# Channel sums on GpSimd ahead of one averaging product, in the inner norm of a retention layer

## The chip, the core and the metric

The kernel runs on one core of a Trainium2 chip. The core has five engines that run side by side and meet at semaphores: TensorE (PE, matrix products into PSUM), VectorE (DVE), ScalarE (ACT), GpSimd (POOL) and SyncE (SP, which issues the DMAs of the activations and the FFN weights here). PE's weight loads are shown apart as PEld. The metric is the time of one execution on the device in microseconds.

## The reference

One layer of attention without softmax ("retention"), and one FFN, each between two norms ("sandwich"). x has 4 x 1024 tokens of 512 channels, all in float32.

- Attention: `xn = layernorm(x)`; q, v and the gate are `xn` times three 512x512 matrices; the state runs along the sequence, `state = lam * state + v`; then `out = q * state`.
- The inner norm, which the change is about: over the 512 channels of each token, `mu = mean(out)`, `var = mean((out - mu)^2)`, `out = (out - mu) * rsqrt(var + 1e-5) * gamma + beta`.
- Then `out * silu(gate)`, a product with Wo, and `x = x + layernorm(that)`.
- FFN: `xn = layernorm(x)`; gate and up project to 1536 with weights rounded to float8 values and scaled per output; `silu(gate) * up` goes back to 512 by a third such matrix; `x = x + layernorm(that)`.

## The kernel before

The 4096 tokens are worked in eight blocks (t = 0 to 7) of 512 tokens, `TB`. Within attention the data lies transposed: channels on the 128 partitions, in NC = 4 chunks, and the 512 tokens of the block along the free dimension. So a chunk of one block is a 128x512 tile.

`retention(t)` is a generator; each `yield` ends a step. Its steps are: two for the first norm and the transposes into `xnT` (L218 to L228), four for the chunks (L232 to L247), one for mu and its subtraction (L248 to L253), one for var and the reciprocal root (L254 to L262), four for the gate (`wg`) and the scaling (L265 to L275), and five for the output projection `po`, the residual and the next norm (L279 to L298). In the step of a chunk c, PE makes `pv` and `pq` (`project`, L200, four products each), DVE scans `pv` along the tokens (L237), keeps the last column in `carry` (L245) and multiplies by `pq` into `y[:, c, :]` (L246).

The mean over channels is a mean over partitions and over the four chunks. It is taken on PE: `mean_w` is a 128x128 matrix filled with 1/512, and the product of it with a chunk puts the chunk's share of the mean on all 128 partitions; the four chunks add up in one PSUM tile:

```python
for c in range(NC):
    nc.tensor.matmul(mu, mean_w, y[:, c, :], start=(c == 0), stop=(c == NC - 1))
```

DVE subtracts mu from the four chunks (L252). For var, ACT squares each chunk into a tile `sq` (L257) and PE takes the same product of it (L258). ACT takes the root of var (L260), which needs a load of another activation table before it and one after it, and DVE the reciprocal (L261).

`ffn(t)` has NI = 12 steps, one for each 128 of the 1536 hidden channels. In a step PE makes the gate and the up product (`project_split`, L209, eight passes each: the input is split into two float32r parts), ACT the silu (L320), DVE the product with up (L321), ACT and DVE split the result into two parts (the cast L323 and the subtraction L324, into `fuse`), and PE then makes the down product of the step before (L310, eight passes). After the twelve steps come the norm and the residual (L332 to L335, with the add on POOL at L334).

`together` weaves the generators: ffn(t) runs its thirteen steps, and after each of them retention(t + 1) makes so many of its seventeen that it ends with the twelfth; that puts the last chunk and mu behind the same FFN step, and var behind the next. retention(0) runs alone. A third generator, `round_weights`, rounds the FFN weights in twelve pieces with DVE and ACT (L148 to L157, 128x1536 each); six pieces go with retention(0), six with ffn(0) and retention(1). From these calls the Tile framework's scheduler makes the final order of each engine's instructions, which can differ from the order of the calls, and puts in the semaphore waits. [...]

Buffers that matter: PSUM has a pool `ps_a` with two banks, in which pv, pq, mu, var, the gate and po take turns, and a pool `ps_f` with two for the FFN's gate and up. In SBUF the tag `ret` has two buffers, for the scan's output and for `sq`; the tag `rstd` has one, for the reciprocal root of a block (read last at L270). POOL has little work: the tiny operations that make a reciprocal root of the token norms (`rstd_of`, L168 and L169) and the two residual adds (L293 and L334).

Of the kernel before, what the change touches and what calls it, by code (L numbers as in the profile page):

```python
# [10 lines left out]
F32 = mybir.dt.float32  # L11
I32 = mybir.dt.int32
F32R = mybir.dt.float32r
AF = mybir.ActivationFunctionType
ALU = mybir.AluOpType

P = 128
# [5 lines left out]
def retention_ffn_sandwich(  # L23
# [19 lines left out]
    nc = tc.nc  # L43
    NT, D = x.shape
    I = gate_w.shape[1]
    NC = D // P
    NI = I // P
    TB = 512
# [7 lines left out]
    work = ctx.enter_context(tc.tile_pool(name="work", bufs=2))  # L56
    small = ctx.enter_context(tc.tile_pool(name="small", bufs=4))
    ps_a = ctx.enter_context(tc.tile_pool(name="ps_a", bufs=2, space=bass.MemoryType.PSUM))
# [59 lines left out]
    mean_w = const.tile([P, P], F32, tag="mean_w", name="mean_w")  # L118
# [42 lines left out]
    def stats(src, mv):  # L161
        st = small.tile([P, 6], F32, tag="st", name="st")
        nc.vector.bn_stats(st, src)  # L163
        nc.vector.bn_aggr(mv, st)  # L164

    def rstd_of(var, n):
        r = small.tile([P, n], F32, tag=f"rstd{n}", name="rstd")
        nc.gpsimd.tensor_scalar(r, var, EPS, 1.0, ALU.add, ALU.mult)  # L168
        nc.gpsimd.tensor_tensor(r, r, nhalf[:, :n], ALU.pow)  # L169
        return r  # L170

    def center_scale(dst, src, mean, rstd):
        nc.vector.tensor_scalar(dst, src, mean, rstd, ALU.subtract, ALU.mult)  # L173

    def norm(dst, src):
        mv = small.tile([P, 2], F32, tag="mv", name="mv")
        stats(src, mv)
        rstd = rstd_of(mv[:, 1:2], 1)
        center_scale(dst, src, mv[:, 0:1], rstd)

    def to_channels(dst, src, s):

        pt = ps_a.tile([P, NC, P], F32, tag="pa", name="pt")
        for c in range(NC):
            nc.tensor.transpose(pt[:, c, :], src[:, ts(c, P)], ident)
        nc.scalar.copy(dst[:, :, ts(s, P)], pt)

    def to_channels_split(hi, lo, src, s):

        pt = ps_a.tile([P, NC, P], F32, tag="pa", name="pt")  # L190
        for c in range(NC):
            nc.tensor.transpose(pt[:, c, :], src[:, ts(c, P)], ident)
        nc.scalar.copy(hi[:, :, ts(s, P)], pt)  # L193
        nc.vector.tensor_tensor(lo[:, :, ts(s, P)], pt, hi[:, :, ts(s, P)], ALU.subtract)  # L194

    def project(pool, tag, w, col, xT):

        po = pool.tile([P, TB], F32, tag=tag, name=f"po_{tag}")
        for c in range(NC):
            nc.tensor.matmul(  # L200
                po, w[:, c, ts(col, P)], xT[:, c, :], start=(c == 0), stop=(c == NC - 1)
            )
        return po
# [11 lines left out]
    def retention(t, give):  # L215
        xt = xs[t]

        mv4 = small.tile([P, NS, 2], F32, tag="mv4", name="mv4")  # L218
        for s in range(NS):
            stats(xt[s], mv4[:, s, :])  # L220
        rstd4 = rstd_of(mv4[:, :, 1], NS)
        xnT = big.tile([P, NC, TB], F32, tag="xnT", name=f"xnT_{t}")
        for s in range(NS):
            xn = work.tile([P, D], F32, tag="tok", name=f"xn_{t}_{s}", bufs=5)
            center_scale(xn, xt[s], mv4[:, s, 0:1], rstd4[:, s : s + 1])
            to_channels(xnT, xn, s)
            if s % 2 == 1:
                yield  # L228


        y = big.tile([P, NC, TB], F32, tag="y", name=f"y_{t}")
        for c in range(NC):  # L232
            pv = project(ps_a, "pa", wv_sb, c, xnT)
            pq = project(ps_a, "pa", wq_sb, c, xnT)
            ret = work.tile([P, TB], F32, tag="ret", name=f"ret_{t}_{c}")
            first = (t * TB) % seq == 0
            nc.vector.tensor_tensor_scan(  # L237
                ret,
                lam[:, c : c + 1].to_broadcast([P, TB]),
                pv,  # L240
                0.0 if first else carry[:, c : c + 1],
                ALU.mult,
                ALU.add,
            )
            nc.vector.tensor_copy(carry[:, c : c + 1], ret[:, TB - 1 : TB])  # L245
            nc.vector.tensor_tensor(y[:, c, :], pq, ret, ALU.mult)  # L246
            yield  # L247
        mu = ps_a.tile([P, TB], F32, tag="pa", name=f"mu_{t}")  # L248
        for c in range(NC):
            nc.tensor.matmul(mu, mean_w, y[:, c, :], start=(c == 0), stop=(c == NC - 1))  # L250
        for c in range(NC):
            nc.vector.tensor_tensor(y[:, c, :], y[:, c, :], mu, ALU.subtract)  # L252
        yield  # L253
        var = ps_a.tile([P, TB], F32, tag="pa", name=f"var_{t}")  # L254
        for c in range(NC):
            sq = work.tile([P, TB], F32, tag="ret", name=f"sq_{t}_{c}")
            nc.scalar.activation(sq, y[:, c, :], AF.Square)  # L257
            nc.tensor.matmul(var, mean_w, sq, start=(c == 0), stop=(c == NC - 1))  # L258
        rstd = work.tile([P, TB], F32, tag="rstd", name=f"rstd_{t}", bufs=1)
        nc.scalar.activation(rstd, var, AF.Sqrt, bias=eps_sb)  # L260
        nc.vector.reciprocal(rstd, rstd)  # L261
        yield  # L262


        for c in range(NC):  # L265
            pg = project(ps_a, "pa", wg_sb, c, xnT)
            g = work.tile([P, TB], F32, tag="sg", name=f"g_{t}_{c}", bufs=3)
            nc.scalar.activation(g, pg, AF.Silu)  # L268
            nc.vector.scalar_tensor_tensor(
                y[:, c, :], y[:, c, :], gamma_sb[:, c : c + 1], rstd, ALU.mult, ALU.mult  # L270
            )
            nc.vector.scalar_tensor_tensor(  # L272
                y[:, c, :], y[:, c, :], lnb_sb[:, c : c + 1], g, ALU.add, ALU.mult
            )
            yield  # L275

        x1nT = big.tile([P, 2, NC, TB], F32R, tag="x1n", name=f"x1nT_{t}", bufs=2)  # L279
        hi, lo = x1nT[:, 0, :, :], x1nT[:, 1, :, :]  # L280
        give((hi, lo))
        before = None
        for s in range(NS):
            po = ps_a.tile([P, D], F32, tag="pa", name=f"po_{t}_{s}")
            for c in range(NC):
                nc.tensor.matmul(  # L286
                    po, y[:, c, ts(s, P)], wo_sb[:, c, :], start=(c == 0), stop=(c == NC - 1)
                )
            if before is not None:
                to_channels_split(hi, lo, before, s - 1)  # L290
            o = work.tile([P, D], F32, tag="tok", name=f"o_{t}_{s}", bufs=5)
            norm(o, po)
            nc.gpsimd.tensor_tensor(xt[s], xt[s], o, ALU.add)  # L293
            before = work.tile([P, D], F32, tag="tok", name=f"x1n_{t}_{s}", bufs=5)
            norm(before, xt[s])
            yield
        to_channels_split(hi, lo, before, NS - 1)
        yield  # L298
# [57 lines left out]
    def start(t):  # L356
        return retention(t, lambda z: given.__setitem__(t, z))
# [57 lines left out]
```

## Time and profile before

| what | value |
|---|---|
| median of 3 runs | 1191.93 us (1189.42 to 1192.23) |
| the profiled execution | 1189.74 us, its span 1188.0 us |
| granted TensorE clock, mean | 0.975 |
| busy: PE / PEld / DVE / ACT / POOL | 1084.3 / 679.4 / 579.7 / 281.4 / 168.8 us |
| an ordinary block's stretch from the mu products to the first gate (`wg`) product | 320.99 to 338.90 us |
| PE's longest waits in all | 27.0 us before the transposes L192, 22.8 us before the transposes L185, 12.3 us before the up product L209 |
| HBM | 26 GB/s over the span |

A busy time is the sum of an engine's instructions; PE's are pipelined and their ends are modelled, so their starts are the better measure. A group of instructions is given as line, engine, operation, output and inputs with shapes, the count, then the busy time in us and the mean in ns, then the idle time of the engine just before such instructions and what ended it. A timeline's line is the start in us, the duration in us, the engine and the operation, `x` the number of instructions merged, and in brackets the idle time before it with its releaser. A float32 product of 128x512 stands in the profile as two records. "Ordinary blocks" below are the six in which no weights are rounded any more, retention(2) to retention(7).

### The profile page before, as it was taken

Reading aid. Unit: us, or ns where it says so; the run is one execution under the profiler, and the core shown is the slowest. Engines: PE = TensorE matmul, PEld = TensorE weight load, DVE = VectorE, ACT = ScalarE, POOL = GpSimd, SP = SyncE. Lnnn points to the kernel's source line nnn. Section 1 sums busy time; section 2 is a strip of 40 time slices with the busy share of each in tenths; the row PEclk is TensorE's granted clock in tenths of the full one; section 3 lists DMA queues with packets and bytes.
Section 4 is the critical chain, followed back from the end, with each engine's and each line's share of the span. In section 5 each row is a group of like instructions: output and inputs, shape, how many; then the busy total and the mean of one; then the engine's idle time right before and its main releaser. Section 6 shows DMA issues by size and latency. Waiting matters only on the chain. (4 is left out here: it accounts for less than half of the span.)

```text
span 1188.0 us, 9580 instructions
## 1 busy us (share of the span) xinstructions
PE 1084.3 (91%) x3712; PEld 679.4 (57%) x3712; DVE 579.7 (49%) x895; ACT 281.4 (24%) x382; POOL 168.8 (14%) x278
## 2 busy tenths in 40 slices
PE   5684999989999899998999989998899979999994
PEld 3232655655666555666566555665566655666683
DVE  3876667564344733456242652436433473335523
ACT  1542435311131212212021120311113111221221
POOL 0003000132001400034000330013100240003302
PEclk9897899999999999999999999999999999999998
DMA  8110011001000100002000020000100010000000
GB/s 283 53 54 26 27 54 54 0 17 55 1 0 1 64 8 0 1 1 71 1 0 1 1 72 0 1 1 28 43 0 1 1 62 1 1 1 0 37 1 35
DMA packets 18127, 31.31 MB, mean 26 GB/s; under 512 B 2081, under 2 KB 6177, under 8 KB 18081
## 3 DMA queue, kind: packets, MB, share of 16 engines
q1 hardware_dynamic: 17216, 30.41, 7.4%
q8 instruction: 29, 0.48, 0.2%
q10 hardware_dynamic: 864, 0.28, 0.1%
q14 instruction: 18, 0.14, 0.0%
HBM read 22.30 MB, written 8.39 MB: 26 GB/s over the span
## 5 line engine op out<-in xcount | busy, mean ns | idle before, releaser
L209 PE MATMUL po_pf<-x1nT,gate_sb 128*128 128x512 f32 x768 | 219.6, 424 | 0.7 <-ACT x1nT L193 0.7
L209 PE MATMUL po_pf<-x1nT,up_sb 128*128 128x512 f32 x768 | 197.8, 396 | 12.3 <-DVE gate L321 12.3
L310 PE MATMUL pd<-down_sb,fuse 128*128 128x512 f32 x768 | 195.5, 394 | 8.6 <-DVE fuse L324 8.6
L209 PEld LDWEIGHTS po_pf<-x1nT,gate_sb 128*128 128x128 f32 x768 | 143.7, 190 | 56.6 <-issue 23.9
L209 PEld LDWEIGHTS po_pf<-x1nT,up_sb 128*128 128x128 f32 x768 | 144.8, 190 | 44.3 <-DVE gate L321 15.2
L310 PEld LDWEIGHTS pd<-down_sb,fuse 128*128 128x128 f32 x768 | 142.8, 189 | 44.6 <-DVE fuse L324 14.8
L168 POOL TENSOR_SCALAR rstd<-mv 128x1 f32<-128x1 f32 (+1 forms) x104 | 24.2, 232 | 953.4 <-DVE mv L164 951.4
L320 ACT ACTIVATE gate<-po_pf,gs_sb 128x512 f32<-128x512 f32 x96 | 66.1, 688 | 281.2 <-PE po_pf L209 281.2
L321 DVE SCALAR_TENSOR_TENSOR gate<-po_pf,us_sb,gate 128x512 f32<-128x512 f32 x96 | 71.1, 740 | 123.0 <-PE po_pf L209 122.0
L200 PE MATMUL po_pa<-xnT,wv_sb 128*128 128x512 f32 x256 | 117.6, 603 | 5.5 <-DVE ret L237 4.8
L286 PE MATMUL po<-wo_sb,y 128*128 128x512 f32 x256 | 118.2, 606 | 2.6 <-DVE x1nT L194 1.4
L200 PE MATMUL po_pa<-xnT,wq_sb 128*128 128x512 f32 x256 | 115.1, 592 | 0.0
L200 PE MATMUL po_pa<-xnT,wg_sb 128*128 128x512 f32 x256 | 113.8, 592 | 0.9 <-ACT rstd L260 0.9
L323 ACT CAST fuse<-gate 128x512 fp32r<-128x512 f32 x96 | 59.5, 620 | 207.6 <-DVE gate L321 178.5
L324 DVE TENSOR_TENSOR fuse<-gate,fuse 128x512 fp32r<-128x512 f32 x96 | 70.0, 730 | 38.5 <-ACT fuse L323 38.5
L200 PEld LDWEIGHTS po_pa<-xnT,wq_sb 128*128 128x128 f32 x256 | 48.6, 190 | 61.2 <-issue 60.7
L200 PEld LDWEIGHTS po_pa<-xnT,wv_sb 128*128 128x128 f32 x256 | 49.3, 193 | 60.1 <-issue 51.7
L286 PEld LDWEIGHTS po<-wo_sb,y 128*128 128x128 f32 x256 | 48.9, 194 | 57.6 <-issue 51.9
L200 PEld LDWEIGHTS po_pa<-xnT,wg_sb 128*128 128x128 f32 x256 | 48.4, 189 | 54.2 <-issue 50.8
L163 DVE BATCH_NORM_STATS2 st<-x 128x6 f32<-128x512 f32 x64 | 42.9, 681 | 42.5 <-POOL x L293 37.7
L169 POOL TENSOR_TENSOR rstd<-rstd,nhalf 128x1 f32<-128x1 f32 (+1 forms) x104 | 60.2, 579 | 8.7
L272 DVE SCALAR_TENSOR_TENSOR y<-y,lnb_sb,g 128x512 f32<-128x512 f32 x32 | 23.9, 750 | 74.0 <-ACT g L268 74.0
(58 smaller groups left out, 798.4 us busy)
## 6 DMA issues: line engine op xcount, KB each, us to landing
x<-in_x SPq DMA_DIRECT2D x32, 256.0 KB, 2.7
out<-d SPq DMA_DIRECT2D x32, 256.0 KB, 2.0
scr<-in_gate_w SPq DMA_DIRECT2D x4, 768.0 KB, 4.6
scr<-in_up_w SPq DMA_DIRECT2D x4, 768.0 KB, 4.7
scr<-in_down_w SPq DMA_DIRECT2D x4, 768.0 KB, 4.5
wv_sb<-in_wvT SPq DMA_DIRECT2D x2, 512.0 KB, 5.5
wq_sb<-in_wqT SPq DMA_DIRECT2D x2, 512.0 KB, 7.2
wg_sb<-in_wgT SPq DMA_DIRECT2D x2, 512.0 KB, 8.1
```

Of the source, the lines that this page charges most:

```text
L163: nc.vector.bn_stats(st, src)
L168: nc.gpsimd.tensor_scalar(r, var, EPS, 1.0, ALU.add, ALU.mult)
L169: nc.gpsimd.tensor_tensor(r, r, nhalf[:, :n], ALU.pow)
L200: nc.tensor.matmul(po, w[:, c, ts(col, P)], xT[:, c, :], start=(c == 0), stop=(c == NC - 1))
L209: nc.tensor.matmul(po, w[:, c, ts(col, P)], part[:, c, :], start=(c == 0 and part is hi), stop=(c == NC - 1 and part is lo),)
L272: nc.vector.scalar_tensor_tensor(y[:, c, :], y[:, c, :], lnb_sb[:, c : c + 1], g, ALU.add, ALU.mult)
L286: nc.tensor.matmul(po, y[:, c, ts(s, P)], wo_sb[:, c, :], start=(c == 0), stop=(c == NC - 1))
L310: nc.tensor.matmul(pds[s], f[:, h, ts(s, P)], down_sb[:, i, :], start=(i == 0 and h == 0), stop=(i == NI - 1 and h == 1),)
L320: nc.scalar.activation(g, pg, AF.Silu, scale=gs_sb[:, i : i + 1])
L321: nc.vector.scalar_tensor_tensor(g, pu, us_sb[:, i : i + 1], g, ALU.mult, ALU.mult)
L323: nc.scalar.copy(f[:, 0, :], g)
L324: nc.vector.tensor_tensor(f[:, 1, :], g, f[:, 0, :], ALU.subtract)
```

## The change

While the chunks are made, POOL adds them up: the first add when the second chunk is ready, then one for each further chunk, into a tile `ysum` that takes the single buffer of the tag `rstd`. mu is then one product of `mean_w` with `ysum`. For var, ACT squares the first chunk straight into a tile `sqsum` (same tag), the other three into `sq` as before; POOL adds these to `sqsum` one after another; var is one product of `mean_w` with `sqsum`. The subtraction, the root and all that follows stay as they are.

```diff
             nc.vector.tensor_copy(carry[:, c : c + 1], ret[:, TB - 1 : TB])
             nc.vector.tensor_tensor(y[:, c, :], pq, ret, ALU.mult)
+            if c == 1:
+                ysum = work.tile([P, TB], F32, tag="rstd", name=f"ysum_{t}", bufs=1)
+                nc.gpsimd.tensor_tensor(ysum, y[:, 0, :], y[:, 1, :], ALU.add)
+            elif c > 1:
+                nc.gpsimd.tensor_tensor(ysum, ysum, y[:, c, :], ALU.add)
             yield
         mu = ps_a.tile([P, TB], F32, tag="pa", name=f"mu_{t}")
-        for c in range(NC):
-            nc.tensor.matmul(mu, mean_w, y[:, c, :], start=(c == 0), stop=(c == NC - 1))
+        nc.tensor.matmul(mu, mean_w, ysum, start=True, stop=True)
         for c in range(NC):
             nc.vector.tensor_tensor(y[:, c, :], y[:, c, :], mu, ALU.subtract)
         yield
-        var = ps_a.tile([P, TB], F32, tag="pa", name=f"var_{t}")
-        for c in range(NC):
+        sqsum = work.tile([P, TB], F32, tag="rstd", name=f"sqsum_{t}", bufs=1)
+        nc.scalar.activation(sqsum, y[:, 0, :], AF.Square)
+        for c in range(1, NC):
             sq = work.tile([P, TB], F32, tag="ret", name=f"sq_{t}_{c}")
             nc.scalar.activation(sq, y[:, c, :], AF.Square)
-            nc.tensor.matmul(var, mean_w, sq, start=(c == 0), stop=(c == NC - 1))
+            nc.gpsimd.tensor_tensor(sqsum, sqsum, sq, ALU.add)
+        var = ps_a.tile([P, TB], F32, tag="pa", name=f"var_{t}")
+        nc.tensor.matmul(var, mean_w, sqsum, start=True, stop=True)
         rstd = work.tile([P, TB], F32, tag="rstd", name=f"rstd_{t}", bufs=1)
         nc.scalar.activation(rstd, var, AF.Sqrt, bias=eps_sb)
         nc.vector.reciprocal(rstd, rstd)
```

## The prediction

> **What bounds the kernel now.** I read the page's busy times first, then the waits of PE, then the costliest groups, then the timeline of one ordinary block. A block here is one turn of retention(t + 1) woven into ffn(t).
>
> ```profile
> PE 1084.3 (91%) x3712; PEld 679.4 (57%) x3712; DVE 579.7 (49%) x895; ACT 281.4 (24%) x382; POOL 168.8 (14%) x278
> ```
>
> PE is busy for 91% of 1188.0 us, and in the window from 320.99 to 338.90 us for all 17.9 us. So in an ordinary block, whatever leaves PE is worth its full time, and whatever makes PE wait costs its full time. POOL does nothing at all in that window. The groups concerned:
>
> ```profile
> L258 PE MATMUL var<-sq,mean_w 128*128 128x512 f32 x64 | 32.0, 639 | 6.0 <-ACT sq L257 6.0
> L250 PE MATMUL mu<-y,mean_w 128*128 128x512 f32 x64 | 29.1, 595 | 1.6 <-DVE ret L237 1.4 <-DVE y L246 0.2
> L293 POOL TENSOR_TENSOR x<-x,o 128x512 f32<-128x512 f32 x32 | 42.4, 1324 | 31.1 <-DVE o L173 31.1
> L334 POOL TENSOR_TENSOR d<-d,x 128x512 f32<-128x512 f32 x32 | 41.4, 1293 | 22.4 <-DVE d L173 9.9 <-issue 9.3 <-DVE mv L164 3.1
> ```
>
> [...]Each f32 product of 128x512 shows as two records (8 blocks x 4 products = 64). They start 0.43 us apart, so the mean of 595 ns overlaps and one product really costs 0.86 us. The waits before mu and var (1.6 and 6.0 us) all fall in the first two blocks; the six ordinary ones have none. The block itself, start and duration first:
>
> ```profile
> 317.56 3.60 PE L200 MATMUL po_pa<-xnT,wq_sb 128*128 128x512 f32 x8
> 320.99 3.60 PE L250 MATMUL mu<-y,mean_w 128*128 128x512 f32 x8
> 321.19 0.69 DVE L246 TENSOR_TENSOR y<-po_pa,ret 128x512 f32<-128x512 f32 x1 [2.02 <-PE po_pa L200]
> 324.02 2.39 PE L209 MATMUL po_pf<-x1nT,gate_sb 128*128 128x512 f32 x8
> 324.62 2.48 DVE L252 TENSOR_TENSOR y<-y,mu 128x512 f32<-128x512 f32 x4 [2.74 <-PE mu L250]
> 325.34 1.23 ACT L257 ACTIVATE sq<-y 128x512 f32<-128x512 f32 x2 [11.36 <-DVE y L252]
> 329.88 3.72 PE L258 MATMUL var<-sq,mean_w 128*128 128x512 f32 x8
> 333.04 2.40 PE L209 MATMUL po_pf<-x1nT,gate_sb 128*128 128x512 f32 x8
> 338.90 7.03 PE L200 MATMUL po_pa<-xnT,wg_sb 128*128 128x512 f32 x16
> ```
>
> See how mu's first three products run while DVE still makes the fourth y chunk, and how var's first two run while ACT squares the rest. The four products cover the latency of their own inputs. One product at the end cannot.
>
> [...]
>
> ```profile
> 111.28 1.75 DVE L157 SCALAR_TENSOR_TENSOR down_sb<-scr 128x1536 fp32r<-128x1536 f32 x1
> 111.45 2.70 POOL L293 TENSOR_TENSOR x<-x,o 128x512 f32<-128x512 f32 x1 [0.93 <-DVE o L173]
> ...
> 409.52 1.28 POOL L334 TENSOR_TENSOR d<-d,x 128x512 f32<-128x512 f32 x1 [0.71 <-issue]
> 409.98 1.37 DVE L324 TENSOR_TENSOR fuse<-gate,fuse 128x512 fp32r<-128x512 f32 x1
> 410.88 0.51 POOL L168 TENSOR_SCALAR rstd<-mv 128x1 f32<-128x1 f32 x1
> ```
>
> The first POOL add took 2.70 instead of 1.28 us behind L157. In the second pair DVE's 0.69 us fuse took 1.37 us behind a POOL add, and the next POOL instruction (0.51 instead of 0.19) then waited for DVE[...]. [...]the trace has 1.28, which I use. [...]no row of before has two such adds chained, so the hand-off between them is my weakest number.
>
> **The change, part by part, in an ordinary block.** *Removed:* 3 of 4 mu products and 3 of 4 var products, 6 x 0.86 = 5.15 us of PE.
>
> *Moved:* in the changed program's order, mu comes after 7 of the 8 first gate products of the next FFN step, and var after the next step's first gate product. The squares no longer straddle the FFN's activation: ACT does gate, four squares, then the fuse cast L323. SP's queue and its DMAs are not passed by anything here.
>
> *Added before mu:* three POOL adds; two are long done, the third follows the last y chunk. y ends at 321.19 + 0.69 = 321.88; the hand-off from DVE to POOL is 0.08 (L173 to L293), the add 1.28, the hand-off to PE taken as 0.06 (the DVE to PE one): mu can start at 323.30. PE reaches it at about 320.99 + 7 x 0.227 = 322.6 (eight gate passes of the split FFN take 1.81 us). PE stops for 0.7 us; queued behind are gate, up and down. mu's result is there about 1.12 us later, at 324.4, so the subtraction starts at 324.45, practically where it was (324.62).
>
> *Added before var:* the subtractions end at 325.1, 325.8, 326.4 and 327.0; the FFN's gate activation goes first on ACT and ends at 325.5, and the squares follow at 0.6 us: 326.1, 326.7, 327.35. The first add runs 326.80 to 328.08. The fourth square needs the buffer of the second (tag ret has two), which that add frees: 328.12 to 328.75. The second add runs 328.16 to 329.44. The cast then ends at 329.37, so DVE's L324, with two SBUF inputs, becomes ready at 329.41, just before the second add ends. [...] The third add then runs 330.1 to 331.4 and var starts at 331.4; were L324 a little later, 330.8. PE arrives at 323.30 + 0.86 + 0.23 + 1.81 + 1.81 + 0.23 = 328.2 and stops for 3.2 us (2.6 without the collision). Behind it stand seven gate products, up and down; they need 331.4 + 0.86 + 7 x 0.227 + 1.81 + 1.81, so wg starts at 337.5 to 337.6 instead of 338.90. Net gain 1.3 us (1.9 without the collision), out of 5.15.
>
> *Costed at nothing:* the earlier y adds (POOL is idle[...]); the cast L323 behind the squares (it starts at 328.75 against 329.12 before, and its fuse is wanted by down only at 335.7; each further wait of the fourth square would move it, with 6 us of cover); the shared rstd buffer (its last reader is a block back); the activation table loads (one pair as before). The root comes at about 332.6 instead of 333.73, so DVE's 3.35 us reciprocal still ends before wg starts. The tail of a block (the transposes' waits) follows PE and shifts with it.
>
> *The second block* (mu at 178.66) also has rounding on DVE. y ends at 180.92, so mu at 182.3; var's third add ends between 189.7 and 191.6 depending on whether L148 and L324 get in between. Against 192.92, where PE had two gate products behind it, that is a gain of 1.6 to 0.65: I take 1.0.
>
> *The first block* has no FFN on PE to cover anything. Before, the last var pass ends at about 65.8. Now the subtractions start at 58.4, the squares end at 62.3, and the second and third adds meet L155 (1.75 us), L148 and L157 on DVE: var ends at 67.7 to 69.4. wg was waiting for the root at 69.42 anyway; with the new ACT order the output projection moves from 79.82 to 81.4 or later, and its first chunk group from 83.3 to 86. I take a loss of 2.5 (1 to 4.3).
>
> Sum: 6 x 1.3 + 1.0 - 2.5 = 6.3 us. The profiled execution took 1189.74 us (span 1188.0), which gives 1183.4. Its runs had a median of 1191.93, 2.2 higher; from there it is 1185.6. I say 1184.5.
>
> **The rivals.** *The adds are hidden* and PE keeps most of it: 8 x 5.15 = 41 us, 1150. POOL is idle there and the program put gate products in front. Against it, from mu's result at 324.4 to the third add's end the chain takes 6.4 to 7.0 us, and PE has only 4.1 us of products there. If L324 slips behind the third add and the hand-offs are quicker, I get at most 2.5 a block: 1172 to 1178.
>
> *No measurable change:* ordinary blocks 1.3 each, but the first block costs 4.3 and the second gives 0.65: 4.1 us, at the edge, or 1 to 3 if each add is 0.1 slower. Measurement tells about 0.3%, 3.6 us.
>
> *Slower:* an add on POOL with its hand-off costs more than the row says. Four adds lie on the path of each ordinary block, one before mu and three before var. With 1.3 us to lose, the sign of a block turns when each takes 0.33 us longer, 1.7 instead of 1.36 from start to start. At 2.0 us a block loses 1.3, and with the first block's 2.5 and the second's, some 11 us: 1202. [...] Against it: consumers of L293 start 0.03 us after its 1.28, and 1.259 is its least.
>
> **How the numbers follow.** The forecast has 0.56, hidden 0.12, no change 0.18, slower 0.14. Forecast and hidden make faster 0.68. The likeliest case alone spans 1180 to 1188 (the two values of the collision and of the first block). For 8 in 10 I go down to 1176, which leaves out about half of the hidden case, and up to 1194, which leaves out about half of the slower one.
>
> **What would show it.** mu and var with 16 records each; PE waiting on POOL before mu by 0.7 and before var by 2.6 to 3.2 us in each of six blocks, some 21 us in all; wg 16.6 instead of 17.9 us after the last wq product; adds at 1.28 us, with L324 between the second and the third; the first block's output projection later. Wrong it would be if POOL's adds chain at other than 1.36 us, if DVE's subtraction collides after all, or if later waits grow or shrink by more than a few us.

## The result, and the profile after

No difference that can be told: 1191.45 us (median of four runs, 1189.34 to 1192.54) against 1190.68 us for the kernel before on the same chip, a ratio of 1.0004 with a 95% interval of 0.9982 to 1.0027. The profiled execution took 1192.22 us, its span is 1190.4 us (before: 1188.0), and the granted clock fell from 0.975 to 0.966. One execution of before_late, an experiment below, ran at a clock of 0.56 from end to end (1871 us) and is left out of its figures.

The page's busy times of the kernel after, and the granted clock in 40 slices of the span (tenths of full speed):

```profile
PE 1055.1 (89%) x3616; PEld 667.5 (56%) x3616; DVE 584.2 (49%) x895; ACT 279.8 (24%) x382; POOL 238.0 (20%) x326
...
PEclk9978799999999999999999999999999999999997
```

Some 41 us of products left PE (8 x 5.15), yet it is busy for only 29.2 us less, and the span is 2.4 us longer. So PE stands still, or runs slower, for as long as it was relieved. The groups of the products and of POOL's adds (after: L254 mu, L265 var, L251 and L263 the new adds, L300 and L341 the residual adds):

```profile
L263 POOL TENSOR_TENSOR sqsum<-sqsum,sq 128x512 f32<-128x512 f32 x24 | 34.9, 1455 | 30.4 <-ACT sq L262 29.1
L251 POOL TENSOR_TENSOR ysum<-ysum,y 128x512 f32<-128x512 f32 x16 | 21.8, 1363 | 175.9 <-DVE y L246 175.9
L254 PE MATMUL mu<-ysum,mean_w 128*128 128x512 f32 x16 | 10.9, 769 | 12.9 <-POOL ysum L251 12.9
L265 PE MATMUL var<-sqsum,mean_w 128*128 128x512 f32 x16 | 10.0, 707 | 24.5 <-POOL sqsum L263 24.5
```

The 64 records of each product have become 16. PE now waits 12.9 us for ysum and 24.5 us for sqsum in the eight blocks together. The same ordinary block as in the prediction, on the timeline of the kernel after (start, duration, and in brackets the idle time before):

```profile
325.47 3.60 PE L200 MATMUL po_pa<-xnT,wq_sb 128*128 128x512 f32 x8
...
329.94 1.28 POOL L251 TENSOR_TENSOR ysum<-ysum,y 128x512 f32<-128x512 f32 x1 [11.04 <-DVE y L246]
331.27 1.12 PE L254 MATMUL mu<-ysum,mean_w 128*128 128x512 f32 x2 [0.60 <-POOL ysum L251]
...
334.46 4.32 POOL L263 TENSOR_TENSOR sqsum<-sqsum,sq 128x512 f32<-128x512 f32 x3 [3.25 <-ACT sq L262]
...
336.96 0.70 DVE L331 TENSOR_TENSOR fuse<-gate,fuse 128x512 fp32r<-128x512 f32 x1 [1.38 <-ACT fuse L330]
...
338.84 1.12 PE L265 MATMUL var<-sqsum,mean_w 128*128 128x512 f32 x2 [2.32 <-POOL sqsum L263]
...
345.06 7.03 PE L200 MATMUL po_pa<-xnT,wg_sb 128*128 128x512 f32 x16
```

From the last wq products to the first wg product it takes 345.06 - 325.47 = 19.59 us; before it took 338.90 - 317.56 = 21.34. The block gains 1.75 us, as the prediction has it (1.3 to 1.9). So the gain of the ordinary blocks is there; it must be lost elsewhere. I compare where wg starts in block after block, after minus before: 6.68 us in the second block, then 6.16, 5.98, 4.47, 4.32, 4.17 and 2.45. The first block loses much more than was allowed for, and the ordinary blocks bring 6.68 - 2.45 = 4.23 us in all instead of 6 x 1.75 = 10.5.

**The first block.** PE's timeline there, first before, then after:

```profile
47.44 3.60 PE L200 MATMUL po_pa<-xnT,wq_sb 128*128 128x512 f32 x8
...
64.08 1.02 PE L200 MATMUL po_pa<-xnT,wg_sb 128*128 128x512 f32 x2
64.94 1.02 PE L258 MATMUL var<-sq,mean_w 128*128 128x512 f32 x2
65.80 2.74 PE L200 MATMUL po_pa<-xnT,wg_sb 128*128 128x512 f32 x6
69.42 10.57 PE L200 MATMUL po_pa<-xnT,wg_sb 128*128 128x512 f32 x24 [0.88 <-ACT rstd L260]
79.82 4.46 PE L286 MATMUL po<-wo_sb,y 128*128 128x512 f32 x10
```

```profile
48.71 3.60 PE L200 MATMUL po_pa<-xnT,wq_sb 128*128 128x512 f32 x8
57.54 2.08 PE L254 MATMUL mu<-ysum,mean_w 128*128 128x512 f32 x2 [5.24 <-POOL ysum L251]
68.71 2.08 PE L265 MATMUL var<-sqsum,mean_w 128*128 128x512 f32 x2 [9.10 <-POOL sqsum L263]
70.58 15.74 PE L200 MATMUL po_pa<-xnT,wg_sb 128*128 128x512 f32 x32
86.16 7.03 PE L293 MATMUL po<-wo_sb,y 128*128 128x512 f32 x16
```

The first block runs 1.27 us later at the wq products already, for reasons of its start (not_first below, whose first block is that of before, begins them at 48.36, between the two). From there to the output projection it took 79.82 - 47.44 = 32.38 us before and 86.16 - 48.71 = 37.45 after: 5.07 more. The bulk of wg starts at nearly the same distance, 21.98 and 21.87 us. But before, 8 of its 32 records were done by then, 8 x 0.43 = 3.4 us of work; and after, PE stood still for 5.24 and 9.10 us, and its granted clock was 0.50 from 57.2 to 74.3 us, so that two records took 2.08 instead of 1.12 us and the 32 took 15.74 instead of 32 x 0.43 = 13.9. These are 3.4 + 1.8 = 5.2 us. (Before had a stretch at a clock of 0.50 here as well, 56.6 to 63.5 us; it lies ahead of the bulk of wg, which comes at the same distance in both.) To the first FFN product the loss grows by another 2.0, with longer waits of the transposes on the way: 71.50 us from wq before, 78.54 after, 7.04 in all.

**The ordinary blocks.** The start of an ordinary block (its transposes) on PE's timeline, before and after:

```profile
418.10 1.17 PE L185 MATMUL pt<-ident,xn 128*128 128x128 f32 x8 [1.83 <-DVE xn L173]
...
420.36 0.70 PE L209 MATMUL po_pf<-x1nT,up_sb 128*128 128x512 f32 x2
420.90 2.00 PE L310 MATMUL pd<-down_sb,fuse 128*128 128x512 f32 x8
...
422.74 1.45 PE L200 MATMUL po_pa<-xnT,wv_sb 128*128 128x512 f32 x3
```

```profile
424.31 1.18 PE L185 MATMUL pt<-ident,xn 128*128 128x128 f32 x8 [1.86 <-DVE xn L173]
...
427.10 1.20 PE L209 MATMUL po_pf<-x1nT,up_sb 128*128 128x512 f32 x2
428.10 2.53 PE L317 MATMUL pd<-down_sb,fuse 128*128 128x512 f32 x8
...
430.47 1.88 PE L200 MATMUL po_pa<-xnT,wv_sb 128*128 128x512 f32 x4
```

Same order, same stop of about 1.85 us, yet from the transposes to wv it takes 6.16 instead of 4.64 us. Busy times and clock in two stretches of the kernel after show why (the eighth number of a row, after POOL's count, is the granted clock):

```profile
core 0: us, PE busy (x) PEld busy (x) DVE busy (x) ACT busy (x) POOL busy (x), PEclk, DMA share, GB/s
422.20:425.60 3.40, 1.54 (x11) 0.99 (x9) 1.98 (x5) 0.60 (x2) 1.22 (x2) 1.00 0.15 53
425.60:429.00 3.40, 3.40 (x14) 2.98 (x14) 0.61 (x2) 1.68 (x3) 0.00 (x0) 0.54 0.00 0
```

A stretch of 3.4 us in which PE is busy for only 1.54 is followed by one of 3.4 us at about half clock (0.54). Every single stretch of this kind in these traces loses 1.70 to 1.71 us of clock, so lasts 3.41 us at a clock of 0.50; the traces of before and after record each as 3413 ns.

When it comes can be counted in the traces. All recorded changes of the clock lie on a grid of 3.413 us. Laid out on this grid, each cell of it called a window, the 13 profiles other than that of before_late have 4175 windows at full clock from the first clock record on (15.7 us in before, 19.7 in after). All 116 with less than 1.55 us of PE work in them were followed by a window at half clock; so were 27 of the 36 with 1.55 to 1.64 us, and none of the 4023 with more. Full clock came back after each of the 130 half-clock windows with 2.82 us of work or more, and after none of the 106 with less. (Work is the busy time of PE's records, whose ends are modelled.) So in these traces the length of a stop did not tell what followed, but the work left in one window did: the stop of 2.32 us before var lies across two windows in every ordinary block of after, leaves 1.57 us or more in each, and brings no half clock there.

I counted these short half-clock stretches by the granted clock in windows of 1 us, between 200 us and the tail of the last block. Before has 3, and one of them, at 268 us, held wg up by only 0.4 us. After has 6, in the same place of each ordinary block. Blocks of after follow each other at 139.98 us, which is 41.0 times 3.413: once the stop lies inside one window it lies there in the next block too. Before's blocks without a stretch take 140.13 us, so there the stop moves by 0.2 us a block against the windows. Two experiments below fit: where each block has a stretch, their blocks follow each other at 143.4 to 143.5 us (before_fill, 42.0 windows) and at 136.4 to 136.6 (not_first_dve, 40.0). That this repetition is what holds the pattern is an inference; that the stretch is there and costs 1.5 us is seen.

Before's 140.13 us less the gain of 1.75 would be 138.38; a block of after takes 1.60 more. Six times that is 9.6 us, where before lost 3.3 to its stretches (0.4, 1.4 and 1.5). The difference, 6.3 us, is what is missing between 10.5 and 4.23.

The account, after minus before: 1.27 (start) + 7.04 (first block) - 1.63 (second block, 8.31 to 6.68) - 4.23 (ordinary blocks) = 2.45 us. The spans differ by 2.4.

### The profile page after: what moved, and what is told of

The parts are those of the page before. It is cut to its first block, busy times and chain, and to the rows that moved or that the text cites. A ratio compares the mean times of both kernels' runs of the same rounds, so it can differ in the third digit from the quotient of the medians.

```text
span 1190.4 us, 9489 instructions
## 1 busy us (share of the span) xinstructions
PE 1055.1 (89%) x3616; PEld 667.5 (56%) x3616; DVE 584.2 (49%) x895; ACT 279.8 (24%) x382; POOL 238.0 (20%) x326
## 5 line engine op out<-in xcount | busy, mean ns | idle before, releaser
L209 PE MATMUL po_pf<-x1nT,gate_sb 128*128 128x512 f32 x768 | 224.6, 428 | 0.7 <-ACT x1nT L193 0.7
L209 PE MATMUL po_pf<-x1nT,up_sb 128*128 128x512 f32 x768 | 199.7, 398 | 12.1 <-DVE gate L328 12.1
L317 PE MATMUL pd<-down_sb,fuse 128*128 128x512 f32 x768 | 198.0, 398 | 9.7 <-DVE fuse L331 9.7
L331 DVE TENSOR_TENSOR fuse<-gate,fuse 128x512 fp32r<-128x512 f32 x96 | 70.1, 730 | 46.3 <-ACT fuse L330 46.3
```

The lines of the kernel that those rows point to most:

```text
L209: nc.tensor.matmul(po, w[:, c, ts(col, P)], part[:, c, :], start=(c == 0 and part is hi), stop=(c == NC - 1 and part is lo),)
L317: nc.tensor.matmul(pds[s], f[:, h, ts(s, P)], down_sb[:, i, :], start=(i == 0 and h == 0), stop=(i == NI - 1 and h == 1),)
L331: nc.vector.tensor_tensor(f[:, 1, :], g, f[:, 0, :], ALU.subtract)
```

## The experiments

Three theories. A: the first block loses some 6 us. The first guess at the cause, an estimate from the trace of after, is twofold: POOL's adds take longer beside DVE's rounding (2.64 instead of 1.28 us), and PE runs at a clock of 0.50 after its stops; a rival cause, that a single product at the end of the chain leaves PE without work there, is tried in the last two experiments. B: a stop of PE of about 2 us can bring a window at half clock; the one ahead of the transposes (1.86 us, then a clock of 0.54) takes back most of what the ordinary blocks gain. C, the rival to both: adds on POOL simply cost as much as they save. Each time is given beside a kernel before on the same chip.

**not_first: the change without the first block.** The first block keeps its eight products.

```diff
+            if t > 0 and c == 1:
...
+        if t > 0:
+            nc.tensor.matmul(mu, mean_w, ysum, start=True, stop=True)
+        else:
+            for c in range(NC):
+                nc.tensor.matmul(mu, mean_w, y[:, c, :], start=(c == 0), stop=(c == NC - 1))
```

and the same for var.

> The new sums only from the second block on; the first block keeps its eight products. Theory A (the first block lost some 6 us: [...]PE, idle for 14 us, comes back at half clock): the gate product of the first block ends about 6 us earlier than in the changed kernel, and the time is 1184 to 1187. Rival (the 8 us by which the changed kernel was late after its first block were an accident of that one execution's start): like the changed kernel, 1190 to 1192.

Measured: 1184.69 us (1184.24 to 1185.04), ratio 0.9955 (0.994 to 0.997). That is 6.8 us below after, and 5.1 us (0.45%) below the kernel before on its chip. From wq to the first FFN product the first block takes 71.3 us (48.36 to 119.67), as before (71.50). Theory A holds in its amount; the cause stays open here. The kernel's ordinary blocks still have one half-clock stretch each, six in all, but in another place: not at the transposes, which run at full clock, but right behind the new stop before var. Its timeline and windows there:

```profile
329.61 1.45 PE L270 MATMUL var<-sqsum,mean_w 128*128 128x512 f32 x2 [2.32 <-POOL sqsum L268]
330.17 3.77 PE L209 MATMUL po_pf<-x1nT,gate_sb 128*128 128x512 f32 x7
```

```profile
326.90:330.30 3.40, 1.08 (x5) 0.46 (x3) 0.70 (x1) 2.08 (x3) 2.57 (x2) 1.00 0.00 0
330.30:333.70 3.40, 3.40 (x9) 2.31 (x8) 1.88 (x1) 1.97 (x2) 0.00 (x0) 0.50 0.02 5
```

Seven gate passes take 3.77 instead of 2.18 us. So the stop that the change itself makes costs 2.32 us and, where it falls into one window, about 1.6 more.

**after_fill, before_fill, not_first_fill: work for PE at the start of a block.** In the ordinary blocks, eight products with a zero matrix (1.8 us) into the down accumulators; nothing is left out.

```diff
+            if i == 1 and 0 < t < NB - 1:
+                for s in range(NS):
+                    for _ in range(2):
+                        nc.tensor.matmul(pds[s], zero, down_sb[:, 0, :], start=False, stop=False)
```

> The changed kernel, plus eight products with a zero matrix (1.8 us of PE, they add zero to the down sums) put into the idle time of PE ahead of the transposes at the start of each of six ordinary blocks. Theory B (PE's idle time there lets the granted clock fall to half for about 3.4 us just after the transposes, which costs 1.6 us in each of six blocks in the changed kernel, and in only some blocks of the kernel before): granted clock 1.00 instead of 0.96 over the 40 us after a block's start, block period 138.4 instead of 140.0 us, 8 to 10 us less than the changed kernel, about 1182. Rival (something else is late there, the clock is only a bystander): the zero products come on top, 0 to 11 us slower than the changed kernel.

> The kernel before with the same zero products. Theory B: it had a falling clock in three of six blocks in the profiled execution, at a cost of 0.4 to 1.6 us each, so it gains some 3 us (1 to 5): 1186 to 1189. Block period 140.1 in all blocks. Rival: 0 to 11 us slower than the kernel before.

> Both: the new sums from the second block on, and the zero products. If A and B both hold, the gains add up: some 15 us less than the changed kernel, 1175 to 1179, and 9 to 11 us (six ordinary blocks at 1.75) plus 1.6 (second block) less than the kernel before with zero products. If only one holds, 1182 to 1187.

Measured: 1208.59 us (ratio 1.0135, 1.0105 to 1.0165), 1206.36 us (1.0136, 1.0118 to 1.0154) and 1198.41 us (1.0054, 1.003 to 1.0078). These lie far above what a half-clock stretch taken away would give, and above the rival's 0 to 11 us as well. The stop did not go:

```profile
421.55 1.18 PE L189 MATMUL pt<-ident,xn 128*128 128x128 f32 x8 [1.81 <-DVE xn L177]
...
422.88 1.77 PE L189 MATMUL pt<-ident,xn 128*128 128x128 f32 x8
```

This is before_fill at a block's start. The DVE work that the transposes wait for follows PE's own products, so the added ones push it back by their whole length: 6 x 1.81 = 10.9 us come on top. The half-clock stretches became more, too, 6 instead of 3 in before_fill (and 12, two a block, in after_fill); at some 1.6 us each, that makes 15.7 of the 17.2 us by which its span grew (1205.2 against 1188.0). This did not test theory B; it only showed that filling is no remedy there.

**before_late and not_first_late: the stop taken away by order.** The next block's token statistics go into the first FFN step, and the rest of its retention starts one FFN step later. The transposes then stand behind a down product, with their inputs long ready.

```diff
+    def ahead(t):
+        first_norm(t)
+        yield
...
-            others.append((start(t + 1), A_STEPS, 1, NI))
+            others.append((ahead(t + 1), 1, 0, 1))
+            others.append((start(t + 1), A_STEPS, 2, NI))
```

`first_norm` holds the lines of `retention` from `mv4` to `rstd4`.

> The kernel before with eight products per block, and one thing else: the statistics of the next block's x are put into the first FFN step, and the rest of the next block's retention starts one FFN step later (17 steps over 10 FFN steps instead of 11). Its transposes then follow the second down product, long after their inputs. It is the measure for not_first_late. Theory B (PE runs at half clock after the transposes because it stood idle for 1.83 us just before them): the idle time before the transposes goes, 7 x 1.83 = 12.8 us, and so does the half-clock stretch in three of six blocks (about 3 us), so 1174 to 1178, and the granted clock over the first 40 us of every ordinary block is 1.00. Rival (the transposes themselves bring the lower clock, or it returns at fixed times): the idle time goes but the clock still falls somewhere in the block start, 1177 to 1181. Third possibility: the retention has one FFN step less to spread over, and its last steps now come late and hold up the next block's start: no gain, 1187 or more.

> The same shift, with the change in blocks 1 to 7 (the first block keeps its eight products). In this order PE has a whole FFN step (gate, up and down, 5.6 us) between mu and var instead of 4.1 us, and mu stands behind a down product. Theory A + B (the product is worth its 5.15 us per block, of which the stops of 0.6 and 2.3 us and the half clock of about 1.6 us after the transposes take back most): with the stops down to about 1 us and no idle time before the transposes, 4.1 us a block stay, 7 x 4.1 = 29 us below before_late, 1143 to 1152. Theory A alone, with the clock still falling at block starts: about 10 us more, 1153 to 1162. Rival (the time is set by DVE, ACT or POOL as soon as PE gets shorter, so that products removed from PE bring nothing more): within 8 us of before_late.

> The kernel of before_late once more, for its timeline, since the profile of before_late fell into a stretch of half clock from end to end. Theory (PE runs for one 3.41 us window at half clock after a window in which it stood still for some 1.8 us or more): no stop of 1.8 us is left at the start of the ordinary blocks, so none of the short half-clock windows that before had there. Rival (the low window comes with the transposes or at fixed times): such windows in some of blocks 2 to 7. The 8 us that before_late lost must show as longer waits of the transposes for x1n in the last steps of a block.

Measured: before_late 1197.3 us (1195.47 to 1198.92 in four executions), ratio 1.0069 (1.0055 to 1.0083); not_first_late 1169.19 us (1167.46 to 1169.95), ratio 0.9831 (0.9818 to 0.9845). before_late_look, one more execution of before_late, took 1198.1 us. PE's waits in it (us in all, times, longest):

```profile
PE pt L192 <- DVE x1n L173: 39.1, 24, 9.0
PE pt L185 <- DVE xn L173: 12.8, 2, 12.3
...
PE pt L185 <- ACT xnT L186: 8.7, 6, 1.5
```

The stop before the transposes fell from 22.8 to 12.8 us (what is left lies in the first two blocks), but the other end of the retention, with less room, lost 39.1 - 27.0 = 12.1 us, and a new wait for ACT's copy 8.7. This is the third possibility of the expectation: the order itself is a loss of 8 us. The half-clock stretches are nevertheless gone: one is left, at 271 us in the second block, behind a stop of 2.04 us, and none in the six ordinary blocks. not_first_late has none from 200 us to the tail. This supports B: take away the stop, and the stretch goes. Waits of 1.5 us before the second transposes brought none here.

Between these two kernels the change in seven blocks is worth 1197.3 - 1169.2 = 28.1 us, 4.0 a block, against 4.1 expected. The time itself is 17 us above the 1143 to 1152 of the expectation, since the order costs time instead of saving it. In this order PE has a whole FFN step between mu and var, and var's stop is 6.6 us in seven blocks:

```profile
PE var L281 <- POOL sqsum L279: 6.6, 7, 2.6
```

So theory C falls: the same adds on POOL save 4.0 us a block where they are covered.

**not_first_mu: the mean's part alone**, in blocks 1 to 7; var keeps its four products.

> Only the mean's part of the change, in blocks 1 to 7: one product for mu from a sum added on GpSimd, and four products for var as before. Theory (the mean's part brings the gain, 2.57 us of products less 0.6 us of stop, and the variance's part brings 2.57 less 2.3 us, about nothing): the time of the version with both parts in blocks 1 to 7, 1184.7, within 2.5 us, and no wait of PE for var in the ordinary blocks. Rival (both parts bring about the same): half the gain, 1187 to 1188.

Measured: 1186.59 us (1184.6 to 1188.94), ratio 0.998 (0.9972 to 0.9988). It lies 1.9 us above not_first, within the theory's 2.5; but beside the kernel before on its own chip it gains 2.7 us, about half of not_first's 5.1, which is the rival's case. The time doesn't decide; the trace does. An ordinary block goes from wq to wg in 19.70 us, against 19.59 with both parts in after, and PE has no wait for var there. (not_first needs 21.2 there, since its half-clock stretch lies in between.) In the ordinary blocks the mean's part brings the gain, and the variance's part nearly nothing, 2.57 us of products for a stop of 2.32. In the second block it is worth 2.2 us: from wq to wg 21.9 us in not_first and 24.1 here.

**not_first_dve and not_first_late_dve: the adds on VectorE.** As not_first and not_first_late, with

```diff
-                nc.gpsimd.tensor_tensor(ysum, ysum, y[:, c, :], ALU.add)
+                nc.vector.tensor_tensor(ysum, ysum, y[:, c, :], ALU.add)
```

in all three places.

> The change in blocks 1 to 7, with its six adds per block on VectorE instead of GpSimd. Theory (the stop of 2.3 us before var is the length of three chained GpSimd adds of 1.28 us, 4.3 us in all, and the stop brings a window of half clock with it): the adds take about 0.69 us, var's stop falls below 0.7 and mu's below 0.3, a block gains 4.2 to 5 instead of 1.75 us, 1155 to 1162; with a half-clock window left at every block's start, 10 us more, 1165 to 1172. Rival (six adds more on VectorE delay its FFN work and the norms, and PE waits for those instead): 1180 or more.

> The same adds on VectorE in not_first_late, whose stop before var is 0.9 us (6.6 us in seven blocks) and which has no half-clock window in ordinary blocks. Theory: only these stops can be gained, less what the later var costs: 1162 to 1168. Rival (VectorE's added 4.2 us a block lie on the path): 1170 or more.

Measured: 1158.84 us (1154.38 to 1160.85), ratio 0.9737 (0.9714 to 0.976), and 1159.77 us (1158.24 to 1161.16), ratio 0.9747 (0.9725 to 0.9768). Both are faster than before and after, and can't be told from each other. The first lies within its forecast; the second lies below its 1162 to 1168. An ordinary block of not_first_dve:

```profile
320.31 0.69 DVE L251 TENSOR_TENSOR ysum<-ysum,y 128x512 f32<-128x512 f32 x1
321.06 1.12 PE L255 MATMUL mu<-ysum,mean_w 128*128 128x512 f32 x2
...
325.28 1.48 DVE L268 TENSOR_TENSOR sqsum<-sqsum,sq 128x512 f32<-128x512 f32 x2
...
327.28 0.68 DVE L268 TENSOR_TENSOR sqsum<-sqsum,sq 128x512 f32<-128x512 f32 x1
...
328.19 1.02 PE L270 MATMUL var<-sqsum,mean_w 128*128 128x512 f32 x2
...
332.27 7.03 PE L200 MATMUL po_pa<-xnT,wg_sb 128*128 128x512 f32 x16
```

The add takes 0.69 us, and mu and var have no stop. From the last wq products (315.95) to wg it takes 16.32 us, 5.02 less than before, nearly all of the 5.15 removed. The six adds cost DVE 4.2 us a block, but DVE is busy for half the span only, and PE's waits for it before the transposes have not grown (26.9 us for x1n, 27.0 in not_first). Five half-clock stretches are left in not_first_dve, one in the second block and four at the transposes. not_first_late_dve has none, and is no faster: its waits for x1n are longer (39.1 against 26.9 us).

**after_first_dve: the first block's adds on VectorE**, all else as after.

> The changed kernel, with the six adds of the first block alone on VectorE; all else as after. Theory of the first block's loss of about 6.3 us: half of it is GpSimd's adds waiting for VectorE's weight rounding [...](2.64 instead of 1.28 us for one, 5.95 instead of 4.0 us for three) and delaying the rounding in turn, so 1187 to 1189.5, 2 to 4 us below after. Rival (the loss is a single product at the end of a chain with nothing else for PE to do, and half clock after it, wherever the adds run): within 1.5 us of after, 1190 to 1193.

Measured: 1190.31 us (1187.76 to 1193.66), ratio 1.0007 (0.9996 to 1.0017): within 1.2 us of after, the rival's case. In after's first block, POOL's adds and DVE's rounding do take longer where they overlap:

```profile
44.35 2.64 POOL L251 TENSOR_TENSOR ysum<-ysum,y 128x512 f32<-128x512 f32 x1 [10.48 <-DVE y L246]
...
62.70 5.95 POOL L263 TENSOR_TENSOR sqsum<-sqsum,sq 128x512 f32<-128x512 f32 x3 [5.22 <-ACT sq L262]
...
67.45 2.82 DVE L157 SCALAR_TENSOR_TENSOR gate_sb<-scr 128x1536 fp32r<-128x1536 f32 x1
```

(in an ordinary block of after the adds take 1.28 and 4.32 us; L157 takes 1.75 us at 59.02, with no POOL add beside it). But on VectorE the second and third var adds come behind the same rounding instead (L157 at 65.70, 1.75 us, and L148 at 67.97, 0.95 us), and var starts 19.70 us after wq, against 20.00. The output projection comes 37.39 us after wq, against 37.45: up to there, the longer adds don't set the loss. Behind it they may have a part: from the projection to the first FFN product it takes 38.2 us here, 41.1 in after and 39.1 in before. Whether that is their doing is not shown.

**after_first_wg: wg before var in the first block.** The four products of the first gate chunk go ahead of var's product; the gate's activation waits for var, through an added bias of zero.

```diff
+        pg0 = project(ps_a, "pa", wg_sb, 0, xnT) if t == 0 else None
         sqsum = work.tile([P, TB], F32, tag="rstd", name=f"sqsum_{t}", bufs=1)
...
-            pg = project(ps_a, "pa", wg_sb, c, xnT)
+            pg = pg0 if t == 0 and c == 0 else project(ps_a, "pa", wg_sb, c, xnT)
```

> The changed kernel, with one thing else in the first block alone: the four products of the first gate chunk (wg) are issued before var's product instead of behind it, and the gate's activation is held until var is there, so that the activation's queue keeps its order. Theory (in the first block the single var product at the end of the chain keeps back the wg products that PE could do meanwhile, as the four-product form let it do, and the empty stretch brings half clock): 3.4 us of wg move into the 9.1 us stop, and the output projection of the first block comes 3.4 to 5 us earlier, 1186 to 1188.5. Rival (the chain from var over the root and the reciprocal to the scaled y sets the first block's end, whatever PE does): within 1.5 us of after, 1190 to 1193.

Measured: 1188.83 us (1186.75 to 1193.16), ratio 0.9996 (0.9985 to 1.0007). The time, 2.6 us below after, lies just outside the theory's range and can't be told from after by itself; the trace can:

```profile
49.04 3.60 PE L200 MATMUL po_pa<-xnT,wq_sb 128*128 128x512 f32 x8
...
59.16 4.77 PE L200 MATMUL po_pa<-xnT,wg_sb 128*128 128x512 f32 x8
68.47 2.07 PE L266 MATMUL var<-sqsum,mean_w 128*128 128x512 f32 x2 [4.54 <-POOL sqsum L264]
71.51 12.36 PE L200 MATMUL po_pa<-xnT,wg_sb 128*128 128x512 f32 x24 [0.97 <-ACT rstd L271]
83.71 7.03 PE L300 MATMUL po<-wo_sb,y 128*128 128x512 f32 x16
```

The stop before var is halved, the output projection comes 34.67 us after wq instead of 37.45 (2.8 us earlier, where 3.4 to 5 were expected), and the first FFN product 74.0 instead of 78.54: 4.5 of the first block's 7.0 us are back. Some of it is lost again to a seventh half-clock stretch, at 280 us.

## Why the prediction was wrong, step by step

- **What bounds the kernel**: right. PE's order carries the time, and what leaves PE without a new stop is gained: 4.0 us of 5.15 a block where the adds are covered, and 5.0 with adds that are quick enough.
- **The ordinary block, removed and added**: right, net 1.75 us against 1.3 to 1.9. mu's stop was 0.60 (0.7 forecast) and var's 2.32 (2.6 to 3.2). The three adds took 4.32 us in all: 334.46 to 335.75, 335.83 to 337.11, and 337.50 to 338.78 (the last from its end and 1.28; its record is 1.59 us long, from 337.19). L331 came between the second and the third, as L324 was expected to (the author's estimate, from two overlaps in the trace of before); it delayed the third by 0.3 us (a gap of 0.39 instead of 0.08), not by 0.6. The new terms stand about where they were put.
- **The second block**: gain 1.63 against 1.0 (0.65 to 1.6).
- **The first block**: the step that failed first. A loss of 2.5 (1 to 4.3) was forecast, and it is 7.0 from wq to the first FFN product. var's end was placed well, at the late end: 67.7 to 69.4 forecast, and 70.8 less the 1.27 of the start, 69.5, measured. What failed is the sentence after it, that wg "was waiting for the root at 69.42 anyway". In the timeline of before, 8 of wg's 32 records were done by 69.42, inside that very wait. The prediction put the loss of this work at nothing. In after, all 32 came behind the single var product, and PE stood still for 9.10 us before it; that is 3.4 us of work done later. The clock of 0.50, up to 74.3 us, added 1.8, and longer waits behind it, whose cause stays open, 2.0.
- **"The tail of a block (the transposes' waits) follows PE and shifts with it"**: the second step that failed. It shifts, but its price is not fixed. A stop of 1.85 us cost 1.5 us more (6.16 instead of 4.64 us from the transposes to wv) where it left 1.54 us of work in one window and half clock followed. Before paid that in two of the ordinary blocks, and a little in a third; after pays it in all six. So 10.5 us of gain became 4.23. By the counts above, which blocks pay goes with where the stops lie in the windows, which the change itself moves; the trace of before showed the price, and 6 x 1.5 = 9 us could have been put into the range.
- **The rivals**: the measured ratio is that of "no measurable change", which was put at 0.18 and for a partly right reason (a first block of 4.3 with ordinary blocks at 1.3). "Hidden" is false for the kernel as changed. "Slower", by adds longer than 1.69 us, is false: in the ordinary blocks they took 1.28. That the measured time lies within the stated 1176 to 1194 is luck: the upper end was left open for slow adds, not for lost wg work or for the clock.

What stays open: the 2.0 us behind the output projection of the first block, and how the clock is decided between 1.55 and 1.64 us of work in a window. The length of a stop alone doesn't tell: 1.80 us brought half clock in before_fill, 1.87 us did not in a block of before, and 2.32 us did in not_first and did not in after.

## What to carry to other kernels

When several products on the bottleneck engine are folded into one at the end of a chain, count what the old ones covered: not only the latency of their own inputs, but the work queued behind them that could run in between. Fold only where something else fills that time (here not in the first block), and do the folding on the engine that ends the chain soonest, even a busier one: with the first block left as it was, the change brought 0.45% with adds of 1.28 us on POOL, and 2.6% with adds of 0.69 us on VectorE. In a kernel like this one, a stop of PE near 2 us should be priced at up to twice its length: 1.85 us cost 1.5 more in after, and 2.32 us cost 1.6 more in not_first.

## What the runs showed of the hardware

- In the 13 profiles counted above, a single half-clock stretch of PE took 3.41 us and lost 1.7 us of clock. Half clock came after each window of 3.413 us at full clock with less than 1.55 us of PE work (116 of 116) and after none with more than 1.64 (0 of 4023), in block after block, up to twelve times in a profile of 1.2 ms (after_fill). It ended after a half-clock window with 2.82 us of work or more (130 of 130; with less, 0 of 106).
- A POOL add of two 128x512 f32 tiles took 1.28 us, and three of them 4.32 us, fed by ACT, in after; the same add took 0.69 us on VectorE in not_first_dve.
- Between two chained POOL adds of after, VectorE's subtraction L331 passed in 0.70 us (336.96), and the next add began 0.39 instead of 0.08 us after the one before; in the first block a POOL add took 2.64 us beside a VectorE instruction of 1.75 us (L157 at 44.12).
